# Layer 3 of a four-layer block: its experts' tokens found by ranks and gathers, a pair of experts at a time, in place of a scattered table of token numbers

## The chip, the cores and the metric

The kernel runs on one core of a Trainium2 chip, as one launch. The metric is the device time of that launch in microseconds. The engines of the core run side by side, each with its own queue of instructions executed in order: PE (matmuls; PEld are its weight loads), DVE (vector work), ACT (activations and copies), POOL (the indirect DMAs of this kernel and some elementwise work) and SP (the plain DMAs). Engines wait for each other and for DMAs by semaphores.

## The reference

`x` has 2048 tokens of 256 numbers. Four layers each add a cross-attention and then a feed-forward part, both on a layernorm of `x`. Only the feed-forward part of layer 3 is touched: 16 experts, two per token, each expert with a capacity of 320 tokens.

```python
logits = x_tokens @ router_w + router_b
vals, idx = jax.lax.top_k(jax.nn.softmax(logits, axis=-1), K)        # K = 2
vals = vals / (jnp.sum(vals, axis=-1, keepdims=True) + 1e-09)
oh_e = jax.nn.one_hot(idx.reshape(NK), E, dtype=x.dtype)             # E = 16
pos = (jnp.cumsum(oh_e, axis=0) * oh_e).sum(axis=1) - 1              # place of a pair in its expert
within = (pos < C).astype(x.dtype)                                   # C = 320
expert_inputs = jnp.zeros((E, C, d)).at[idx_flat, pos_c].add(x_pair) # slots of each expert
expert_outputs = jax.vmap(_mlp)(expert_inputs, w_gate, w_up, w_down) # silu(h @ wg) * (h @ wu) @ wd
gathered = expert_outputs[idx_flat, pos_c] * (vals_flat * within)[:, None]
output_tokens = gathered.reshape(N, K, d).sum(axis=1)
return x + _mlp(x, sw_gate, sw_up, sw_down) + output_tokens.reshape(b, s, d)
```

So each of the 16 x 320 slots has to learn which token stands in it, and each token has to learn in which two slots its results are.

## The kernel before

Tokens are handled in four blocks of 512 (`NB`), each of four tiles of 128 (`NT`), so 16 tiles. Activations stay in SBUF; the layernormed tokens of layer 3 are also written to HBM (`xn_dram`, L1449), from where rows can be gathered. Within the attention of every layer the order of PE, DVE and ACT is written out by hand. Outside it, in `ffn3` too, a scheduler orders the instructions of each engine: program order gives the priority, and an instruction that is ready may fill a gap. Tiles come from pools; those with the same tag share a fixed number of buffers, and a new one waits until an old one has been read for the last time. PSUM tiles (`ps_one`, `ps_misc`) share seven buffers. `act` tiles tagged `xnT` share five, `work` six, `xn` one.

The end of the program runs as follows. The last block leaves attention (L355 to L380), is normed on DVE and POOL (L393 to L406), transposed (L416), and its router logits are computed (L621); its routing (L746 to L760, L631, L632) runs on DVE. Then `ffn3`:

- Counting. `both` (L1218) is the one-hot of a token's two experts. Two matmuls count, for each token and expert, the earlier tokens of the same tile (`upper`, L1221) and the totals of each tile (`ones`, L1222). DVE sums the totals over the tiles (L1226), and picks each token's place (`pos`, L1242).
- The table. From the place DVE works out a row in a table of token numbers in HBM (L1250 to L1262), and POOL writes the numbers there with 32 indirect DMAs of 128 rows, one for each tile and choice (L1264). SP reads the table back into `slots` (L1280).
- The shared MLP, `mlp_hidden` (L1305 on PE, Silu on ACT L1309, the product on DVE L1312) and its down projection (L1323, L1331), over the four blocks.
- The experts, one after the other: weights by SP (L1290 to L1293, two buffers each), three gathers of token rows by POOL with `slots` (L1338), six transposes on PE (L1348) with copies on ACT (L1351), `mlp_hidden` on 320 columns, the down projection (L1357), its copy (L1364) and its write to `ys_dram` (L1365).
- The combine: for each tile two gathers from `ys_dram` (L1372), two weighted sums on DVE (L1378), and the result of each block to HBM (L1381).

Layer 1 (`ffn1`) has no table: it writes the ranks of tokens within each tile to HBM, finds for each slot the tile that holds its token from the running totals, gathers that tile's row of ranks, and counts how many are not above the slot's rank (L1002 to L1047).

Of the kernel before, what the change touches and what calls it, by code (L numbers as in the profile page):

```python
# [11 lines left out]
F32 = mybir.dt.float32  # L12
# [54 lines left out]
def block_stack(ctx: ExitStack, tc: tile.TileContext, I: dict, out: bass.AP):  # L67
# [1136 lines left out]
    def ffn3(xnT, chosen, xn_dram):  # L1204
        NTT = NB * NT
        TW = E3 * len(SC)

        table = dram.tile([P * TW, 1], I32, name="table")
        zero = const.tile([P, TW], I32, name="zero")
        nc.vector.memset(zero, 0)  # L1210
        nc.sync.dma_start(table.rearrange("(p c) o -> p (c o)", p=P), zero)
        ids = const.tile([P, NTT], I32, name="ids")
        nc.gpsimd.iota(ids, pattern=[[P, NTT]], base=0, channel_multiplier=1)

        oh, idx, w = chosen

        both = act.tile([P, NTT, E3], F32, tag="mp", name="both")
        nc.vector.tensor_tensor(both, oh[0], oh[1], ALU.add)  # L1218
        bothf = both.rearrange("p t e -> p (t e)")
        pin, ptot = ps_one(), ps_one()  # L1220
        nc.tensor.matmul(pin[:, 0 : NTT * E3], upper, bothf, start=True, stop=True)  # L1221
        nc.tensor.matmul(ptot[:, 0 : NTT * E3], ones, bothf, start=True, stop=True)  # L1222
        base = act.tile([P, NTT, E3], F32, tag="mp", name="base")
        nc.vector.memset(base[:, 0, :], 0.0)
        for t in range(1, NTT):
            nc.vector.tensor_tensor(  # L1226
                base[:, t, :], ptot[:, (t - 1) * E3 : t * E3], base[:, t - 1, :], ALU.add
            )
        before = act.tile([P, NTT, E3], F32, tag="mp", name="before")
        nc.vector.tensor_tensor(  # L1230
            before, pin[:, 0 : NTT * E3].rearrange("p (t e) -> p t e", e=E3), base, ALU.add
        )

        def s16(name):
            return small.tile([P, NTT], F32, tag=name, bufs=1, name=name)

        prod = act.tile([P, NTT, E3], F32, tag="mp", name="prod")
        wk, rows = [], []
        for k in range(2):
            nc.vector.tensor_tensor(prod, before, oh[k], ALU.mult)  # L1240
            pos = s16(f"pos{k}")
            nc.vector.tensor_reduce(pos.unsqueeze(2), prod, AX.X, ALU.add)  # L1242
            within = s16(f"within{k}")
            nc.vector.tensor_scalar(within, pos, float(CAP), None, ALU.is_lt)
            wt = s16(f"wt{k}")
            nc.vector.tensor_tensor(wt, w[k], within, ALU.mult)
            wk.append(wt)

            c1, c2 = s16("c1"), s16("c2")
            nc.vector.tensor_scalar(c1, pos, float(P), None, ALU.is_ge)  # L1250
            nc.vector.tensor_scalar(c2, pos, float(2 * P), None, ALU.is_ge)
            nc.vector.tensor_tensor(c1, c1, c2, ALU.add)
            at = s16(f"at{k}")
            nc.vector.tensor_scalar(at, c1, 1.0 - P * TW, None, ALU.mult)
            nc.vector.scalar_tensor_tensor(at, pos, float(TW), at, ALU.mult, ALU.add)
            nc.vector.scalar_tensor_tensor(at, idx[k], float(len(SC)), at, ALU.mult, ALU.add)
            past = s16("past")
            nc.vector.tensor_scalar(past, within, -1e6, 1e6, ALU.mult, ALU.add)
            nc.vector.tensor_tensor(at, at, within, ALU.mult)
            nc.vector.tensor_tensor(at, at, past, ALU.add)  # L1260
            at_u = small.tile([P, NTT], U32, tag=f"at_u{k}", bufs=1, name=f"at_u{k}")
            nc.vector.tensor_copy(at_u, at)  # L1262
            for t in range(NTT):
                nc.gpsimd.indirect_dma_start(  # L1264
                    out=table,
                    out_offset=bass.IndirectOffsetOnAxis(ap=at_u[:, t : t + 1], axis=0),
                    in_=ids[:, t : t + 1],
                    in_offset=None,
                    bounds_check=P * TW - 1,
                    oob_is_err=False,  # L1270
                )

            row = s16(f"row{k}")
            nc.vector.tensor_scalar(row, pos, float(CAP - 1), None, ALU.min)
            nc.vector.scalar_tensor_tensor(row, idx[k], float(CAP), row, ALU.mult, ALU.add)
            row_u = small.tile([P, NTT], U32, tag=f"row_u{k}", bufs=1, name=f"row_u{k}")
            nc.vector.tensor_copy(row_u, row)
            rows.append(row_u)
        slots = small.tile([P, E3, len(SC)], U32, tag="slots", bufs=1, name="slots")
        nc.sync.dma_start(  # L1280
            slots.rearrange("p e c -> p (e c)"),
            table.rearrange("(p c) o -> p (c o)", p=P).bitcast(U32),
        )
# [12 lines left out]
        def mlp_hidden(gu, xT, n):  # L1296
# [3 lines left out]
            for f, (lo, hi) in enumerate(FC):  # L1300
                fw = hi - lo
                pg = [ps_one("ps_h") for i in range(2)]
                for i in range(2):
                    for c in range(2):
                        nc.tensor.matmul(  # L1305
                            pg[i][0:fw, 0:n], gu[:, i, c, lo:hi], xT[:, c, 0:n], start=(c == 0), stop=(c == 1)
                        )
# [7 lines left out]

        gu, dn = load_mlp("sw")
        for b in range(NB):
            hs = mlp_hidden(gu, xnT[b], BT)
# [14 lines left out]
        ys_dram = dram.tile([E3 * CAP, D], F32, name="ys")  # L1333
        for e in range(E3):
            gu, dn = load_mlp("w", e)
            xg = act.tile([P, len(SC), D], F32, tag="work", bufs=6, name="xg")
            for s, (lo, hi) in enumerate(SC):
                nc.gpsimd.indirect_dma_start(  # L1338
                    out=xg[0 : hi - lo, s, :],
                    out_offset=None,  # L1340
                    in_=xn_dram,
                    in_offset=bass.IndirectOffsetOnAxis(ap=slots[0 : hi - lo, e, s : s + 1], axis=0),
                )
            xT = act.tile([P, 2, CAP], F32, tag="work", bufs=6, name="xT")
            for c in range(2):
                pt = ps_misc()
                for s, (lo, hi) in enumerate(SC):
                    nc.tensor.transpose(  # L1348
                        pt[:, lo:hi], xg[0 : hi - lo, s, c * P : (c + 1) * P], ident[0 : hi - lo, 0 : hi - lo]
                    )  # L1350
                nc.scalar.copy(xT[:, c, :], pt[:, 0:CAP])  # L1351
            hs = mlp_hidden(gu, xT, CAP)
            ys = act.tile([P, len(SC), D], F32, tag="o_tok", bufs=2, name="ys_sb")
            for s, (lo, hi) in enumerate(SC):
                pd = ps_one()
                for f, (flo, fhi) in enumerate(FC):
                    nc.tensor.matmul(  # L1357
                        pd[0 : hi - lo, 0:D],
                        hs[f][:, lo:hi],
# [221 lines left out]
```

## Time and profile before

| | us |
|---|---|
| median of three runs | 4492.72 (4482.02 to 4495.58) |
| profiled execution | 4487.74 |
| its span, first to last instruction | 4486.0 |
| PE busy in the span | 4258.6 (95%) |
| DVE, ACT, POOL busy | 2414.3, 1959.6, 653.1 |
| shared MLP of layer 3 | 4141.5 to 4205.7 |
| first expert's first transpose | 4237.9 |
| combine and output | 4434 to 4486.0 |

A line of the profile names the source line, the engine, the operation, the tile written and the tiles read, their shapes and a count; times are microseconds from the start of the span, durations of a single instruction are in ns where that is said. What stands after a bar or in brackets is the time for which the engine was idle just before, with what ended that idle time. The granted PE clock is a share of full speed. A float32 matmul is two PE instructions; a transpose is one.

### The profile page before, as it was taken

Reading aid. Unit: us, or ns where it says so; the run is one execution under the profiler, and the core shown is the slowest. Engines: PE = TensorE matmul, PEld = TensorE weight load, DVE = VectorE, ACT = ScalarE, POOL = GpSimd, SP = SyncE. Lnnn points to the kernel's source line nnn. Section 1 sums busy time; section 2 is a strip of 40 time slices with the busy share of each in tenths; the row PEclk is TensorE's granted clock in tenths of the full one; section 3 lists DMA queues with packets and bytes.
Section 4 is the critical chain, followed back from the end, with each engine's and each line's share of the span. In section 5 each row is a group of like instructions: output and inputs, shape, how many; then the busy total and the mean of one; then the engine's idle time right before and its main releaser. Section 6 shows DMA issues by size and latency. Waiting matters only on the chain. (4 is left out here: it accounts for less than half of the span.)

```text
span 4486.0 us, 62975 instructions
## 1 busy us (share of the span) xinstructions
PE 4258.6 (95%) x25100; PEld 1965.4 (44%) x25100; DVE 2414.3 (54%) x4911; ACT 1959.6 (44%) x3690; POOL 653.1 (15%) x833
## 2 busy tenths in 40 slices
PE   8999999999999999998996999999999999998695
PEld 4333333366543333336885433334443333333463
DVE  5776776324677776753222544451486777673122
ACT  1666655511156655662221234343016766665010
POOL 2000100100000010004445100012000001001323
PEclk8999999999999999999998799999899999999897
DMA  2000000000000000002453000000000000000144
GB/s 75 3 3 4 3 3 6 3 23 1 3 3 6 4 8 3 11 6 70 163 167 89 10 5 3 5 6 3 3 16 3 4 3 8 11 1 10 32 148 116
DMA packets 64429, 117.31 MB, mean 26 GB/s; under 512 B 20110, under 2 KB 41478, under 8 KB 59528
## 3 DMA queue, kind: packets, MB, share of 16 engines
q1 hardware_dynamic: 43272, 58.12, 4.3%
q0 software_dynamic: 20864, 55.18, 4.1%
q8 instruction: 198, 3.24, 0.3%
q14 instruction: 95, 0.78, 0.1%
HBM read 138.37 MB, written 16.88 MB: 35 GB/s over the span
## 5 line engine op out<-in xcount | busy, mean ns | idle before, releaser
L284 DVE TENSOR_REDUCE mx<-ps_m 128x1 f32<-128x512 f32 x2688 | 1699.9, 685 | 672.2 <-PE ps_m L277 437.5
L325 PE MATMUL ps_s<-q,kT 32*128 32x512 f32 (+2 forms) x5824 | 1721.0, 623 | 0.7 <-DVE mx L284 0.6
L277 PE MATMUL ps_m<-kT,q 32*128 32x512 f32 x5376 | 1604.8, 644 | 29.9 <-DMA q<-qc 18.5
L335 ACT ACTIVATE e<-ps_s 128x512 f32<-128x512 f32 (+1 forms) x2080 | 1110.7, 599 | 890.5 <-PE ps_s L325 694.4
L343 PE MATMUL ps_acc<-e,V 128*32 128x512 f32 (+2 forms) x5824 | 928.5, 609 | 6.2 <-ACT a L524 5.7
L325 PEld LDWEIGHTS ps_s<-q,kT 32*128 32x128 f32 (+2 forms) x5824 | 576.4, 180 | 671.7 <-DVE mx L284 397.0
L277 PEld LDWEIGHTS ps_m<-kT,q 32*128 32x128 f32 x5376 | 580.4, 188 | 504.4 <-issue 383.1
L333 ACT ACTIVATE e<-ps_s,mcol 128x512 f32<-128x512 f32 (+1 forms) x832 | 514.8, 686 | 224.3 <-PE ps_s L325 143.8
L343 PEld LDWEIGHTS ps_acc<-e,V 128*32 128x32 f32 (+2 forms) x5824 | 160.6, 112 | 640.6 <-issue 508.4
L266 POOL MEMSET mp<- 128x512 f32 x64 | 33.2, 525 | 1846.7 <-PE ps_m L315 1836.2
L1075 ACT ACTIVATE h<-ps_h,w 128x128 f32<-128x128 f32 x320 | 91.1, 372 | 217.7 <-issue 138.2
L854 DVE SCALAR_TENSOR_TENSOR x<-ps_m,cw,x 128x256 f32<-128x256 f32 x256 | 111.1, 479 | 102.1 <-PE ps_m L846 99.1
L402 POOL TENSOR_SCALAR rs<-mv 128x4 f32<-128x4 f32 x32 | 7.6, 239 | 1050.5 <-DVE mv L394 1050.5
L406 POOL TENSOR_SCALAR xn<-x,mv,rs 128x256 f32<-128x256 f32 x128 | 156.0, 1231 | 3.5
L1067 PE MATMUL ps_h<-xT,w 128*128 128x128 f32 x1280 | 153.2, 279 | 0.4 <-issue 0.4
L817 ACT ACTIVATE h<-ps_h 128x512 f32<-128x512 f32 x80 | 47.7, 597 | 242.3 <-PE ps_h L816 242.3
L1067 PEld LDWEIGHTS ps_h<-xT,w 128*128 128x128 f32 x1280 | 149.6, 195 | 0.8 <-issue 0.5
L301 DVE TENSOR_REDUCE mx<-ps_m 128x4 f32<-128x260 f32 x224 | 80.4, 423 | 126.0 <-PE ps_m L293 126.0
L1089 PE MATMUL ps_m<-w,h 128*128 128x256 f32 x640 | 144.6, 379 | 0.0
L1089 PEld LDWEIGHTS ps_m<-w,h 128*128 128x128 f32 x640 | 118.6, 190 | 14.5
L1312 DVE TENSOR_TENSOR h<-ps_h,sg 128x320 f32<-128x320 f32 (+3 forms) x60 | 31.8, 530 | 168.1 <-PE ps_h L1305 121.6
L816 PE MATMUL ps_h<-xnT,up 128*128 128x512 f32 x256 | 117.9, 604 | 0.0
(286 smaller groups left out, 3179.6 us busy)
## 6 DMA issues: line engine op xcount, KB each, us to landing
q<-qc SPq DMA_DIRECT2D x192, 32.0 KB
gu<-in_w_gate SPq DMA_DIRECT2D x16, 352.0 KB
gu<-in_w_up SPq DMA_DIRECT2D x16, 352.0 KB
ys_dram<-ys SPq DMA_DIRECT2D x40, 128.0 KB
xn_dram<-xn SPq DMA_DIRECT2D x8, 512.0 KB
dn<-in_w_down SPq DMA_DIRECT2D x16, 256.0 KB
ys<-ys_sb SPq DMA_DIRECT2D x32, 128.0 KB
x<-in_x SPq DMA_DIRECT2D x4, 512.0 KB
```

Source lines behind the costliest of these rows:

```text
L277: nc.tensor.matmul(pm, q1[at : at + 32, t * P : (t + 1) * P], kT[at : at + 32, g, KB[kb] : KB[kb + 1]], start=True, stop=True,)
L284: nc.vector.tensor_reduce(mx[:, t, j, kb : kb + 1], pm, AX.X, ALU.max)
L325: nc.tensor.matmul(sp, kT[j * S : (j + 1) * S, g, c * P : c * P + cw], q2[j * S : (j + 1) * S, :], start=True, stop=True,)
L333: nc.scalar.activation(e[0:cw], sp, AF.Exp, bias=mcol[0:cw, c : c + 1])
L335: nc.scalar.activation(e[0:cw], sp, AF.Exp)
L343: nc.tensor.matmul(acc[j * S : (j + 1) * S, :], V[0:cw, c, h * (d + 1) : h * (d + 1) + S], es[j // 2][0:cw, j % 2, :], start=(c == 0), sto ...
L406: nc.gpsimd.tensor_scalar(xn[:, t, :], x[b][:, t, :], mv[:, t, 0:1], rs[:, t : t + 1], ALU.subtract, ALU.mult)
L816: nc.tensor.matmul(pu, u(c), xnT[b][:, c, :], start=(c == 0), stop=(c == 1))
L854: nc.vector.scalar_tensor_tensor(x[b][:, t, :], pd[:, i * D : (i + 1) * D], cws[b][:, t, e0 + e + i : e0 + e + i + 1], x[b][:, t, :], ALU. ...
L1067: nc.tensor.matmul(pu[:, (f - f0) * P : (f - f0 + 1) * P], w1[:, c * F1 + f * P : c * F1 + (f + 1) * P], xT[:, c, :], start=(c == 0), stop ...
L1075: nc.scalar.activation(h[:, f, :], pu[:, (f - f0) * P : (f - f0 + 1) * P], AF.Gelu, bias=w1[:, 2 * F1 + f : 2 * F1 + f + 1],)
L1089: nc.tensor.matmul(pd[:, 0:D], h[:, f, :], w2[:, f * D : (f + 1) * D], start=(f == 0), stop=(f == 7))
```

## The change

The table, its 32 scatters, the slots and their arithmetic go. All small tiles are cut from one tile `pad3`, which takes the buffer of layer 3's values (`V`). The counting moves into `counts()`, which also makes the rank of every token in its tile and expert (128 ranks for each of 256 pairs of tile and expert) and writes them to HBM. The 5120 slots are seen as 40 columns of 128, five columns for each pair of experts, the middle column half and half. `locate()` finds for all of them at once the tile and the rank within it; `fetch_ranks(k)` gathers the rank rows of pair k, five indirect DMAs; `tokens(k)` counts along them and gives token numbers; `pairs(k)` gathers the tokens, again five indirect DMAs; `pairs_T` transposes them. These steps stand between the blocks of the shared MLP and then run ahead inside a loop over eight pairs of experts. Each token's own place and weight (`places`) are worked out after experts 3 and 5. The combine and the loads of weights stay as they were.

```diff
     SC = [(0, P), (P, 2 * P), (2 * P, CAP)]
     def ffn3(xnT, chosen, xn_dram):
-        NTT = NB * NT
-        TW = E3 * len(SC)
-        table = dram.tile([P * TW, 1], I32, name="table")
-        zero = const.tile([P, TW], I32, name="zero")
-        nc.vector.memset(zero, 0)
-        nc.sync.dma_start(table.rearrange("(p c) o -> p (c o)", p=P), zero)
-        ids = const.tile([P, NTT], I32, name="ids")
-        nc.gpsimd.iota(ids, pattern=[[P, NTT]], base=0, channel_multiplier=1)
...
         oh, idx, w = chosen
+        vw = 16 * (D // 16 + 1)
+        pad, used = big.tile([P, NCH, vw + P // 4 - D // 16 - 1], F32, tag="V", name="pad3"), 0
+        pad = pad.rearrange("p c n -> p (c n)")
...
+        bothf = cut(NE)
+        nc.vector.tensor_tensor(by_tile(bothf), oh[0], oh[1], ALU.add)
+        ranks_dram = dram.tile([NE, P], F32, name="ranks3_dram")
+        ranks, cum, before = cut(2 * P), by_tile(cut(NE)), by_tile(cut(NE))
+        def counts():
+            for k in range(2):
+                prow, at = ps_one(), slice(k * P, (k + 1) * P)
+                nc.tensor.matmul(prow[:, 0:P], bothf[:, at], upper, start=True, stop=False)
+                nc.tensor.matmul(prow[:, 0:P], bothf[:, at], ident, start=False, stop=True)
+                nc.scalar.copy(ranks[:, at], prow[:, 0:P])
+                nc.sync.dma_start(ranks_dram[at, :], ranks[:, at])
+            ptot, pin = ps_one(), ps_one()
+            nc.tensor.matmul(ptot[:, 0:NE], ones, bothf, start=True, stop=True)
+            nc.tensor.matmul(pin[:, 0:NE], upper, bothf, start=True, stop=True)
+            tot, pin = by_tile(ptot[:, 0:NE]), by_tile(pin[:, 0:NE])
+            nc.vector.tensor_copy(cum[:, 0, :], tot[:, 0, :])
+            for t in range(1, NTT):
+                nc.vector.tensor_tensor(cum[:, t, :], tot[:, t, :], cum[:, t - 1, :], ALU.add)
+            nc.vector.tensor_copy(before[:, 0, :], pin[:, 0, :])
+            nc.vector.tensor_tensor(before[:, 1:, :], pin[:, 1:, :], cum[:, :-1, :], ALU.add)
+        PARTS = [
+            (slice(0, 2), slice(0, P), 0),
+            (slice(2, 3), slice(0, HP), 0),
+            (slice(2, 3), slice(HP, P), 1),
+            (slice(3, 5), slice(0, P), 1),
+        ]
+        rank, tile_of, last, row = (cut(NC) for _ in range(4))
+        row_u, tok_u = cut(NC, U32), cut(NC, U32)
+        gone, cumt = cut(NC * NTT), cut(NC * NTT)
...
+        nc.vector.tensor_copy(rank, slot_id[:, 0:NC])
+        for k in range(E // 2):
+            for cs, ps_, two in PARTS:
+                cols = slice(5 * k + cs.start, 5 * k + cs.stop)
+                nc.gpsimd.tensor_scalar(
+                    rank[ps_, cols], slot_id[ps_, cols], float(-CAP * (2 * k + two)), None, ALU.add
+                )
+                nc.gpsimd.memset(row[ps_, cols], float(2 * k + two))
+        def locate():
+            g4 = gone.rearrange("p (k c t) -> p k c t", c=5, t=NTT)
+            c4 = cumt.rearrange("p (k c t) -> p k c t", c=5, t=NTT)
+            cum4 = cum.rearrange("p t (k two) -> p two k t", two=2)
+            for cs, ps_, two in PARTS:
+                n = cs.stop - cs.start
+                shape = [ps_.stop - ps_.start, E // 2, n, NTT]
+                nc.vector.tensor_tensor(
+                    g4[ps_, :, cs, :],
+                    cum4[ps_, two].unsqueeze(2).to_broadcast(shape),
+                    fives(rank)[ps_, :, cs].unsqueeze(3).to_broadcast(shape),
+                    ALU.is_le,
+                )
+                nc.vector.tensor_tensor(
+                    c4[ps_, :, cs, :],
+                    cum4[ps_, two].unsqueeze(2).to_broadcast(shape),
+                    g4[ps_, :, cs, :],
+                    ALU.mult,
+                )
+            g3 = gone.rearrange("p (c t) -> p c t", t=NTT)
+            c3 = cumt.rearrange("p (c t) -> p c t", t=NTT)
+            nc.vector.tensor_reduce(tile_of.unsqueeze(2), g3, AX.X, ALU.add)
+            nc.vector.tensor_reduce(last.unsqueeze(2), c3, AX.X, ALU.max)
+            nc.vector.tensor_tensor(rank, rank, last, ALU.subtract)
+            nc.vector.tensor_scalar(tile_of, tile_of, NTT - 1.0, None, ALU.min)
+            nc.vector.scalar_tensor_tensor(row, tile_of, float(E), row, ALU.mult, ALU.add)
+            nc.vector.tensor_copy(row_u, row)
+        def fetch_ranks(k):
+            rk = act.tile([P, 5, P], F32, tag="xn", bufs=1, name="rk")
+            for c in range(5):
+                nc.gpsimd.indirect_dma_start(
+                    out=rk[:, c, :],
+                    out_offset=None,
+                    in_=ranks_dram,
+                    in_offset=bass.IndirectOffsetOnAxis(ap=row_u[:, 5 * k + c : 5 * k + c + 1], axis=0),
+                )
+            return rk
+        def tokens(k, rk):
+            at = slice(5 * k, 5 * k + 5)
             nc.vector.tensor_tensor(
...
+                rk, rk, rank[:, at].unsqueeze(2).to_broadcast([P, 5, P]), ALU.is_le
             )
+            tok = tmp([5], "tok5")
+            nc.vector.tensor_reduce(tok.unsqueeze(2), rk, AX.X, ALU.add)
+            nc.vector.scalar_tensor_tensor(tok, tile_of[:, at], float(P), tok, ALU.mult, ALU.add)
+            nc.vector.tensor_scalar(tok, tok, T - 1.0, None, ALU.min)
+            nc.vector.tensor_copy(tok_u[:, at], tok)
+        def pairs(k):
+            xg = [act.tile([P, n, D], F32, tag="xnT", bufs=5, name="xg") for n in (3, 2)]
+            xg = [xg[c // 3][:, c % 3, :] for c in range(5)]
+            for c in range(5):
+                nc.gpsimd.indirect_dma_start(
+                    out=xg[c],
+                    out_offset=None,
+                    in_=xn_dram,
+                    in_offset=bass.IndirectOffsetOnAxis(ap=tok_u[:, 5 * k + c : 5 * k + c + 1], axis=0),
+                )
+            return xg
+        def pairs_T(xg):
+            xT = [wide("xT")[:, 0 : 2 * CAP] for c in range(2)]
+            for c in range(2):
+                for lo, hi in ((0, 4), (4, 5)):
+                    pt = ps_misc()
+                    for col in range(lo, hi):
+                        nc.tensor.transpose(
+                            pt[:, (col - lo) * P : (col - lo + 1) * P], xg[col][:, c * P : (c + 1) * P], ident
+                        )
+                    nc.scalar.copy(xT[c][:, lo * P : hi * P], pt[:, 0 : (hi - lo) * P])
+            return xT
+        def places(k):
...
+            nc.vector.tensor_scalar(wt, pos, float(CAP), None, ALU.is_lt)
+            nc.vector.tensor_tensor(wt, w[k], wt, ALU.mult)
+            nc.vector.tensor_scalar(row_k, pos, float(CAP - 1), None, ALU.min)
+            nc.vector.scalar_tensor_tensor(row_k, idx[k], float(CAP), row_k, ALU.mult, ALU.add)
+            nc.vector.tensor_copy(row_ku, row_k)
+            return wt, row_ku
...
                         nc.tensor.matmul(
-                            pg[i][0:fw, 0:n], gu[:, i, c, lo:hi], xT[:, c, 0:n], start=(c == 0), stop=(c == 1)
+                            pg[i][0:fw, 0:n], gu[:, i, c, lo:hi], xT[c][:, 0:n], start=(c == 0), stop=(c == 1)
...
+        rks, xgs = {}, {}
         gu, dn = load_mlp("sw")
         for b in range(NB):
-            hs = mlp_hidden(gu, xnT[b], BT)
+            if b == 1:
+                counts()
+                locate()
+                rks[0] = fetch_ranks(0)
+            elif b == 2:
+                tokens(0, rks.pop(0))
+                xgs[0] = pairs(0)
+                rks[1] = fetch_ranks(1)
+            elif b == 3:
+                tokens(1, rks.pop(1))
+            hs = mlp_hidden(gu, [xnT[b][:, c, :] for c in range(2)], BT)
...
-        ys_dram = dram.tile([E3 * CAP, D], F32, name="ys")
-        for e in range(E3):
-            gu, dn = load_mlp("w", e)
...
+        ys_dram = dram.tile([E * CAP, D], F32, name="ys")
+        prods = cut(NE)
+        found = {}
+        for k in range(E // 2):
+            xT = pairs_T(xgs.pop(k))
+            if k + 1 < E // 2:
+                xgs[k + 1] = pairs(k + 1)
+            if k + 2 < E // 2:
+                rks[k + 2] = fetch_ranks(k + 2)
+            for two in range(2):
+                e = 2 * k + two
+                gu, dn = load_mlp("w", e)
+                hs = mlp_hidden(gu, [xT[c][:, two * CAP : (two + 1) * CAP] for c in range(2)], CAP)
+                ys = act.tile([P, len(SC), D], F32, tag="o_tok", bufs=2, name="ys_sb")
...
+                if two == 0 and k + 2 < E // 2:
+                    tokens(k + 2, rks.pop(k + 2))
+                if e in (3, 5):
+                    found[(e - 3) // 2] = places((e - 3) // 2)
```

## The prediction

> **What bounds the kernel now.** I first read the busy time by stage of the end of the kernel: the last attention steps, the shared MLP of layer 3, the wait, the experts, the combine. Columns: stretch, its length, then busy us (and instructions) of PE, PEld, DVE, ACT and POOL, the granted PE clock, DMA share, GB/s.
>
> ```profile
> 4115.00:4141.00 26.00, 12.75 (x55) 9.90 (x56) 8.24 (x47) 4.34 (x7) 8.46 (x7) 0.72 0.06 20
> 4141.00:4206.00 65.00, 64.72 (x194) 35.83 (x193) 20.51 (x70) 7.15 (x12) 21.52 (x22) 0.98 0.04 12
> 4206.00:4238.00 32.00, 0.09 (x1) 0.10 (x2) 0.45 (x1) 0.00 (x0) 12.38 (x13) 0.54 0.07 18
> 4238.00:4434.00 196.00, 194.12 (x768) 126.14 (x768) 43.56 (x96) 34.46 (x80) 42.39 (x46) 0.98 0.45 130
> 4434.00:4486.00 52.00, 0.00 (x0) 0.00 (x0) 15.74 (x33) 0.00 (x0) 30.91 (x32) 0.53 0.41 123
> ```
>
> PE fills the shared MLP and the experts; between them it does nothing for 32 us. PE's own timeline shows both holes around the change (start, us, line, then idle before and what ended it):
>
> ```profile
> 4130.78 3.66 PE L621 MATMUL ps_m<-wr,xnT 128*128 128x16 f32 x16 [0.46 <-ACT xnT L417]
> 4139.69 1.19 PE L1221 MATMUL ps_m<-both,upper 128*128 128x256 f32 x2 [5.25 <-DVE base L1224]
> ...
> 4141.53 11.51 PE L1305 MATMUL ps_h<-xnT,gu 128*128 128x512 f32 x24
> ...
> 4200.11 5.61 PE L1323 MATMUL ps_m<-dn,h 128*128 128x256 f32 x24
> 4237.91 0.69 PE L1348 MATMUL ps_m<-ident,xg 128*128 128x128 f32 x2 [32.18 <-DMA xg<-xn_dram,slots]
> ```
>
> What PE waits for is on POOL: 32 scatters into the table, each begun only when the one before has landed, some 2.4 us apart (4150 to 4231), then the read-back of the slots, then the gather.
>
> ```profile
> 4227.73 0.97 POOL L1264 DMA_INDIRECT table<-ids,at_u  x1 [1.40 <-DMA table<-ids,at_u]
> 4230.07 0.97 POOL L1264 DMA_INDIRECT table<-ids,at_u  x1 [1.38 <-DMA table<-ids,at_u]
> 4234.68 1.01 POOL L1338 DMA_INDIRECT xg<-xn_dram,slots  x1 [3.64 <-DMA slots<-table]
> ```
>
> The chain that ended last gives one steady expert, all PE: 1.15 + 6.70 + 4.09 = 11.93 us.
>
> ```profile
> 4254.43 1.15 PE ps_m L1348 x6
> 4255.57 6.70 PE ps_h L1305 x24
> 4262.27 4.09 PE ps_m L1357 x18
> ```
>
> Last, layer 1 already finds tokens by ranks and gathers, so prices for the new work stand in this trace:
>
> ```profile
> L1028 POOL DMA_INDIRECT rk<-ranks_dram,pad x40: 942/964/975, 2077.3 to 2359.6; - x40
> L1034 DVE TENSOR_TENSOR rk<-rk,pad x10: 691/692/694, 2086.9 to 2365.1; 128x512 f32<-128x512 f32 x10
> L1038 DVE TENSOR_REDUCE tok<-rk x10: 674/686/686, 2087.6 to 2366.1; 128x4 f32<-128x512 f32 x10
> ```
>
> **The Trainium skill.** "DMA: Bandwidth & Descriptors", Anatomy of one DMA, puts about 2.0 us of fixed cost, mostly completion, on a DMA that POOL issues; the scatters land in 2.07 us, agreed. The same page, Two DMAs through the same engine are not ordered: a dependent DMA must wait for the first one's semaphore. That is the 1.40 us wait before each scatter, since all write one table; gathers into different columns carry none (issues 1.25 us apart in the combine). "TensorE: Matmul & The Clock Gate", Part 1: an idle PE drops to half clock until about 3.4 us of activity; the trace grants 0.54 in the hole.
>
> **The change part by part.** Measured from the span of 4486.0 us.
>
> Hole before the shared MLP. Today the two count products L1221 and L1222 stand ahead of block 0 on PE and wait 5.25 us for the routing of the last block. After, `counts()` stands behind block 0 in program order, which PE follows in this stage. Block 0 then starts when L621 ends, 4134.4, instead of 4141.5. Its inputs are there: the weights were issued at 3328, xnT of block 0 is old, and ACT's Silu table (4136.8) is in before the first product pair is finished (4134.4 + 3.5). A block costs 15.75 us warm (L1305 starts at 4158.32, 4174.07, 4189.81); block 0 took 16.8 and I keep 0.5 of that 1.05 for a cold clock.
>
> `counts()` on PE. Four rank products of 128 columns, two instructions each: 8 x 0.12 (L1067: 153.2 us for 1280 instructions of 128 columns) = 1.0; two of 256 columns, 4 x 0.227 (4.09 / 18) = 0.9. So 1.9 us. The shared MLP ends at 4134.4 + 4 x 15.75 + 0.5 + 1.9 = 4199.9, instead of 4205.7.
>
> Hole after it. The gap is gone if the first pairs have landed by 4199.9. Counts end at 4152.6. DVE: 16 sums of 16 columns 3.1 (15 took 3.09) and `before`; 4155.8. `locate()`: eight tensor_tensor, 4 x 0.42 (as L1240, 128x256) + 4 x 0.29 (as L640, 128x128) = 2.8; two reductions over 640, (640+151)/0.96 = 0.82 each (estimate by "VectorE: DVE Perf Modes", TRN2 errata; it gives 0.69 at 512, as the trace has); six small ones 1.0; 4161.3. In the same time ACT copies two rank rows (0.3 each), and SP, idle from 4130 to 4200, writes them; the weights of expert 1 stand behind them there, first due at 4195. `fetch_ranks(0)`: five gathers 1.25 apart, the last landing 3.1 after its start (chain: xg 4237.26, 3.10 us): 5.0 + 3.1 = 8.1; 4169.7. `tokens(0)`: 2 x 0.82 + 3 x 0.17 = 2.2; `pairs(0)`: 8.1; landed near 4180.5, 19 us early. Layer 1 needs 36 us from `both` (2057.9) to its first transposes (2093.6); from 4150.7 that is 4187, still early. So the 32.2 us go. What is removed from the chain is POOL's 80 us of scatters (32 x 2.4, a few longer), SP's read-back (1.63) and some 30 DVE instructions of 0.17 between 4147 and 4151.5; only the hole of it was on PE's path, the rest lay under the shared MLP. Expert 0 also ran cold and waited 1.0 for its third gather: 4237.9 to 4254.4 = 16.5 against 11.93, another 4.5 us.
>
> Experts. Transposes fall from 12 to 10 per pair, 0.19 each (1.14/6): a pair costs 10 x 0.19 + 2 x (6.70+4.09) = 23.48 instead of 23.87; eight pairs 187.8, ending at 4387.7. Cover for the rest: POOL 10 gathers per pair, 12.5 us of 23.5 (now 6, 7.5 us); DVE `tokens` 2.2 us per pair, `places` twice some 2 us, while DVE is 22% busy there. PE stays busy as long as h is ready by L1357, 4.5 us after it could be. Weights are issued at the end of L1305 of the expert two before, 17 us ahead of use, and the DMA traffic of one expert lasts some 9 of its 12 us. Without cover each us is paid once per pair.
>
> Sixty-four small POOL writes into `rank` and `row`. No row shows them at this shape; nearest are a 2x16 memset 0.12 and a 128x4 tensor_scalar 0.23, so 8 to 15 us. They need layer 3's V freed (4115). Behind the residual add (4132) they cost 0. If the scheduler puts all ahead of rs (4123.3), into POOL's 8.3 idle us, they delay the last xn by up to 7 us; not below 0. I take 0.
>
> DVE beside the shared MLP: about 14 us added, 2 at most spilling to PE in one block (h waits, seven PSUM buffers). I take 1 for it and the experts' first pair together. The combine keeps its 32 gathers: 52.2 us.
>
> Sum: end of the shared MLP 4205.7 to 4199.9 (start -7.1, cold clock -0.6, counts +1.9) -5.8; hole -32.2; expert 0 -4.5; transposes -3.1 (8 x 0.39); friction +1: -44.6, say -45. Span 4441. The execution took 4487.74, 1.7 more than its span, so 4443; the median of the runs shown is 5 us above it. Against the mean of all four (4489.5) it is 4444.5, against the median 4447.7; I say 4446.
>
> **Rivals.**
> A, more. PE also pulls block 0 into its idle 4121.3 to 4126.0, ahead of L416: 4.7 us more, 4441. Against: now too nothing ready is pulled there or into the 5.25 us.
>
> B, part given back. POOL's small writes ahead of rs (up to 7), DVE late with h at each of three blocks (2 each), PSUM waits in `pairs_T`, which takes four buffers at once (1 per pair): up to 20 back, 4452 to 4470. For: DVE fills gaps out of program order. Against: it has 70% free.
>
> C, slower. DVE runs in order; `tokens(k+2)` stands between the two experts of a pair and can hold up the odd expert's h while ranks are on their way. Layer 1 shows DVE waiting for ranks 52.6 us in 9 waits (5.8 each), though PE isn't held there. Up to 3.5 us late costs nothing; beyond it each us costs six (tokens 2 to 7). It eats the 45 when ranks come 7.5 + 3.5 = 11 us late, i.e. 24 us after the pair's start. Even if POOL starts both groups only at that start, they land after 10 x 1.25 + 3.1 = 15.6, 3 us after the even expert ends. At 14 us late: 6 x 10.5 = 63 lost, 45 won, some 4509.
>
> D, no effect. The small tiles are all cut from one tile; if gathers that read one column held DVE's writes to the next, the chain would slip: the first 19 us are free, then each costs one, and 19 + 45 = 64 us of slip end at some 4491. Layer 1 cuts its tiles the same way and doesn't slip.
>
> **How the numbers follow.** Forecast 0.74 (own range 4434 to 4456, run spread of +-6 included), A 0.06, B 0.11, C 0.05, D 0.04. Range 4432 to 4464: the forecast, A and half of B. 0.3% of 4490 is 13.5 us, about what a measurement can tell from no change. Faster 0.91, same 0.04 (D), slower 0.05 (C).
>
> **What would show it.** L1305 of block 0 straight after L621 with no 5 us hole; POOL with no chained scatters, rank gathers of pair 0 near 4162 to 4170; first expert transposes within 1 us of the last L1323, granted clock near 1.0 there; pairs 23.5 us apart; combine 52 us. Wrong if PE waits over 5 us before the experts, or odd experts' L1357 wait for DVE.

## The result, and the profile after

The changed kernel takes 4495.99 us (median of 20, 4490.11 to 4509.57) against 4487.9 us (20 runs, 4476.28 to 4496.36) for the kernel before: a ratio of 1.0021, 95% interval 1.0012 to 1.0030. It is 8 us slower, where 45 us less were forecast (4446 us). The loss is small, though the interval leaves out 1; the gain isn't there at all, and the forecast is wrong. The profiled execution has a span of 4488.4 us.

Spans differ by some us between executions before the part that was changed is reached. So stages are compared from one mark, the start of the last attention value product (L343), at 4113.05 in the trace of before and 4107.59 after. From there to the end before takes 372.95 us and after 380.81: 7.9 us more, the same as the medians say.

Busy time by stage of the changed kernel: stretch, its length, busy us (and instructions) of PE, PEld, DVE, ACT and POOL, granted PE clock, DMA share, GB/s. The first four rows are blocks 0 to 3 of the shared MLP, then pairs 0 and 1, pairs 2 to 7, the combine.

```profile
4134.50:4151.00 16.50, 16.50 (x47) 9.20 (x48) 7.09 (x38) 3.33 (x5) 0.00 (x0) 0.91 0.01 1
4152.80:4169.10 16.30, 15.75 (x50) 8.80 (x49) 13.35 (x49) 1.79 (x3) 4.15 (x5) 1.00 0.12 20
4169.10:4200.70 31.60, 18.45 (x50) 10.70 (x49) 7.36 (x15) 1.79 (x3) 16.63 (x18) 0.78 0.39 53
4200.70:4231.00 30.30, 19.46 (x49) 10.97 (x48) 7.53 (x15) 1.79 (x3) 14.40 (x16) 0.77 0.47 65
4231.00:4277.00 46.00, 28.61 (x108) 17.93 (x105) 12.10 (x28) 5.44 (x14) 22.93 (x26) 0.85 0.53 104
4277.00:4437.00 160.00, 159.55 (x646) 107.80 (x646) 39.58 (x90) 26.78 (x66) 17.71 (x19) 0.99 0.46 130
4437.00:4488.40 51.40, 0.00 (x0) 0.00 (x0) 15.82 (x33) 0.00 (x0) 30.56 (x32) 0.54 0.43 124
```

The stage of 32 us in which PE did nothing is gone, but blocks 2 and 3 take twice their 15.75 us and pairs 0 and 1 are long too. In those stretches DVE is busy for a quarter of the time. It isn't short of time; it stands still. PE's timeline of the changed kernel (start, us, line, idle before and what ended it) says for what PE waits:

```profile
4124.63 0.69 PE L416 MATMUL ps_m<-ident,xn 128*128 128x128 f32 x2 [7.71 <-POOL xn L406]
...
4193.57 7.27 PE L1414 MATMUL ps_m<-dn,h 96*128 96x256 f32 x20 [13.15 <-DVE h L1392]
...
4221.63 1.22 PE L1414 MATMUL ps_m<-dn,h 128*128 128x256 f32 x2 [10.06 <-DVE h L1392]
...
4231.06 1.25 PE L1346 MATMUL ps_m<-ident,xg 128*128 128x128 f32 x10
...
4254.62 4.83 PE L1441 MATMUL ps_m<-dn,h 96*128 96x256 f32 x10 [12.05 <-DVE h L1392]
...
4277.16 7.88 PE L1385 MATMUL ps_h<-xT,gu 128*128 128x320 f32 x22 [3.81 <-DVE ys_sb L1448]
```

The fourth line is the step forecast: the experts' first transposes follow the shared MLP without a gap. The second, third and fifth wait for `h`, the product of DVE behind which the down projection stands. The sixth waits for a PSUM buffer, which DVE's copy of the results of expert 1 (L1448) frees. The first, for xn, comes last below. DVE's own timeline in block 2 shows why `h` is late:

```profile
4176.25 1.29 DVE L1392 TENSOR_TENSOR h<-ps_h,sg 128x512 f32<-128x512 f32 x2
...
4190.56 0.82 DVE L1318 TENSOR_TENSOR rk<-rk,pad 128x640 f32<-128x640 f32 x1 [13.03 <-DMA rk<-ranks_dram,pad]
...
4192.82 0.69 DVE L1392 TENSOR_TENSOR h<-ps_h,sg 96x512 f32<-96x512 f32 x1
```

The third `h` of block 2 stands behind L1318, the first instruction of `tokens(1)`, and that waits 13.03 us for rank gathers. The inputs of that `h` were there at 4179.5. In the source `tokens(1)` stands after block 2; the scheduler put it between the second and the third `h` of that block. All eight, `tokens(0)` to `tokens(7)`, begin between 4173.6 and 4276, while the source has the last one in pair 5. The list of waits of the changed kernel from 4110 on (waiting for what: us in total, times, longest):

```profile
DVE rk L1318 <- DMA rk<-ranks_dram,pad: 64.9, 8, 13.7
...
PE ps_m L1414 <- DVE h L1392: 24.5, 4, 13.2
...
PE ps_m L1441 <- DVE h L1392: 12.1, 1, 12.1
```

These waits for `h`, the 3.81 us for the copy and 1.5 us for another such buffer make 41.9 us of PE's time. The rest of the 54 us lost against the ordered run below is a lower clock: it was 0.77 to 0.85 in blocks 2 and 3 and pairs 0 and 1, and 20 products took 7.27 us in block 2 where 24 took 5.61 in block 0. Once the eighth is done the pairs follow each other every 22.83 us (23.48 forecast). Last, POOL's timeline of the changed kernel, on the small writes:

```profile
4109.55 3.00 POOL L1273 MEMSET pad<- 128x2 f32 x32 [0.25 <-PE ps_acc L343]
...
4113.13 8.68 POOL L1270 TENSOR_SCALAR pad<-slot_id 64x1 f32<-64x1 f32 x30 [0.20 <-POOL pad L1270]
4121.89 0.23 POOL L402 TENSOR_SCALAR rs<-mv 128x4 f32<-128x4 f32 x1
```

They stand ahead of `rs` of the last block, which sets xn and so L416.

### The profile page after: what moved, and what is told of

The parts are those of the page before. It is cut to its first block, busy times and chain, and to the rows that moved or that the text cites. A ratio compares the mean times of both kernels' runs of the same rounds, so it can differ in the third digit from the quotient of the medians.

```text
span 4488.4 us, 63027 instructions
## 1 busy us (share of the span) xinstructions
PE 4257.7 (95%) x25092; PEld 1972.4 (44%) x25092; DVE 2431.6 (54%) x4946; ACT 1956.7 (44%) x3692; POOL 660.1 (15%) x896
## 5 line engine op out<-in xcount | busy, mean ns | idle before, releaser
L343 PE MATMUL ps_acc<-e,V 128*32 128x512 f32 (+2 forms) x5824 | 925.4, 608 | 5.7 <-ACT a L524 5.7
L343 PEld LDWEIGHTS ps_acc<-e,V 128*32 128x32 f32 (+2 forms) x5824 | 159.9, 112 | 635.5 <-issue 505.7
L846 PE MATMUL ps_m<-dn,h 128*128 128x256 f32 x512 | 117.3, 382 | 0.0
```

Source lines behind the costliest of these rows:

```text
L343: nc.tensor.matmul(acc[j * S : (j + 1) * S, :], V[0:cw, c, h * (d + 1) : h * (d + 1) + S], es[j // 2][0:cw, j % 2, :], start=(c == 0), sto ...
L846: nc.tensor.matmul(pd[:, i * D : (i + 1) * D], h[:, i, t * P : (t + 1) * P], dn[:, e + i, :], start=True, stop=True,)
```

## The experiments

The theory, T: the loss is one of order on DVE's queue. Each `tokens(k)` that stands ahead of an `h` due earlier makes that `h`, and PE, wait for gathers that nothing else needs so soon. Rival W: DVE's added work (or PSUM) is what costs. Rival G: the rank gathers are slow, or held to one buffer's round trip, wherever `tokens(k)` stands. Stages measured from the mark, one profiled execution each, in us:

| | mark to experts | experts to end | mark to end | against after |
|---|---|---|---|---|
| before | 124.9 | 248.1 | 372.95 | -7.9 |
| after | 123.5 | 257.3 | 380.8 | |
| ordered on DVE | 92.5 | 234.0 | 326.5 | -54.3 |
| ordered in the blocks alone | 110.1 | 269.3 | 379.4 | -1.4 |
| ordered in the pairs alone | 109.4 | 234.3 | 343.6 | -37.2 |
| no rank gathers | 93.2 | 232.2 | 325.4 | -55.4 |
| second rank buffer | 134.3 | 233.9 | 368.2 | -12.6 |
| ordered on POOL | 111.2 | 283.4 | 394.6 | +13.8 |
| ordered, tokens(2) early | 104.7 | 234.0 | 338.7 | -42.1 |
| ordered, no small writes | 89.3 | 234.2 | 323.5 | -57.3 |

### Program order on DVE

```diff
+        with tc.manual_schedule(engines={mybir.EngineType.DVE}):
             for b in range(NB):
...
+        with tc.manual_schedule(engines={mybir.EngineType.DVE}):
             for k in range(E // 2):
```

> The changed kernel, but VectorE keeps program order in the shared MLP loop and in the loop over pairs, so tokens(k) stands where the source has it and not ahead of h products that are due earlier. Theory T (order): the 31 us lost in blocks 2 and 3 and the 23 us lost in pairs 0 and 1 come from h standing in VectorE's queue behind a tokens(k) whose ranks are still on their way. Then PE's waits for h (24.5 us at L1414, 12.1 us at L1441 in the changed kernel) fall below 4 us together, blocks take 16 us, every pair 22.8 to 23.5 us, and the time is 4435 to 4455 us, 0.988 to 0.992 of before. Rival W (VectorE's added work or PSUM): the same work is still there, blocks 2 and 3 keep about 30 us, 4488 to 4500. Rival G (the gathers are slow wherever tokens stands): about half of the waits stay, 4465 to 4490.

Measured: 4436.98 us, 0.9893 of before (0.9876 to 0.9909). All instructions are those of the changed kernel; DVE's order differs, and with it how POOL's gathers of ranks and of xg mix. Its stages from block 0 on:

```profile
4136.30:4152.85 16.55, 16.55 (x47) 9.19 (x48) 7.09 (x38) 3.33 (x5) 0.00 (x0) 0.90 0.01 1
4154.60:4170.40 15.80, 15.80 (x49) 8.69 (x48) 11.23 (x35) 1.79 (x3) 4.19 (x5) 1.00 0.13 20
4170.40:4186.15 15.75, 15.75 (x49) 8.82 (x48) 5.49 (x10) 1.79 (x3) 8.02 (x9) 1.00 0.38 57
4186.15:4201.90 15.75, 15.75 (x49) 8.77 (x48) 5.49 (x10) 1.79 (x3) 8.47 (x10) 1.00 0.45 85
4201.90:4224.65 22.75, 22.73 (x95) 15.43 (x93) 7.78 (x17) 4.03 (x10) 8.21 (x10) 1.00 0.62 151
4224.65:4384.40 159.75, 159.61 (x659) 108.41 (x658) 51.61 (x123) 28.19 (x70) 46.98 (x50) 1.00 0.59 147
4384.40:4435.90 51.50, 0.10 (x1) 0.00 (x0) 15.93 (x33) 0.00 (x0) 30.41 (x32) 0.54 0.44 126
```

PE is full in every stage before the combine, at full clock from block 1 on, and no wait of PE for `h` is left. `tokens(1)` still waits 4.81 us for its ranks, and the first two `h` of block 3 stand behind it, but they are done at 4195.4, and PE comes to their down projection at 4196.5, a margin of 1 us; from `tokens(2)` on the ranks have landed before DVE arrives. DVE's timeline of this kernel in pair 0:

```profile
4214.04 0.42 DVE L1450 COPY ys_sb<-ps_m 64x256 f32<-64x256 f32 x1 [1.01 <-PE ps_m L1443]
4214.38 0.81 DVE L1318 TENSOR_TENSOR rk<-rk,pad 128x640 f32<-128x640 f32 x1
...
4216.62 0.49 DVE L1392 TENSOR_TENSOR h<-ps_h,sg 128x320 f32<-128x320 f32 x1
```

W wanted all the waits to stay and G half of them; both fall. All 54.3 us lost against this run, 30.9 in the shared MLP and 23.4 in the pairs, were lost to the order on one engine.

### Without the rank gathers

```diff
-            for c in range(5):
-                nc.gpsimd.indirect_dma_start(
-                    out=rk[:, c, :],
...
-                rk, rk, rank[:, at].unsqueeze(2).to_broadcast([P, 5, P]), ALU.is_le
+                rk, ranks[:, 0:P].unsqueeze(1).to_broadcast([P, 5, P]), rank[:, at].unsqueeze(2).to_broadcast([P, 5, P]), ALU.is_le
```

> Leaves out the 40 rank gathers: tokens(k) compares rows of ranks that lie in SBUF already, the same 128x640 comparison, so the token numbers are other ones. VectorE's work is unchanged, and the scheduler may place it as it likes (it puts all eight tokens(k) among blocks 1 to 2). Theory T: no wait of VectorE for a DMA between the counts and the experts; h is late only by the 18 us of token work that stand ahead of it, of which at most 10 reach PE in blocks 1 and 2; pairs 22.8 us each; 4435 to 4460. Rival W: PE waits for h as in the changed kernel, 20 us or more in the blocks, 4480 to 4500. Rival G: as T, so that this run tells W alone apart.

Measured: 4439.68 us, 0.9900 (0.9884 to 0.9917). DVE does the same token work, all eight pulled ahead once more, without anything to wait for. PE's wait for `h` in the list of waits of this kernel:

```profile
PE ps_m L1407 <- DVE h L1385: 0.8, 1, 0.8
```

So token work placed early is harmless; what costs is a token step that waits. That rules W out a second time, and by another way than the order.

### A second buffer for the ranks

```diff
-            rk = act.tile([P, 5, P], F32, tag="xn", bufs=1, name="rk")
+            rk = act.tile([P, 5, P], F32, tag="xn", bufs=1, name="rk") if k % 2 == 0 else gone.rearrange(
+                "p (c n) -> p c n", c=5
+            )
```

> The ranks of odd pairs land in a second buffer (the 640 columns of gone, free after locate()), so that the rank gathers of pair k+1 need not wait for tokens(k). The scheduler now puts all eight tokens(k) ahead of the last h product of block 3. Theory T: a second buffer doesn't mend it: the last h of block 3 stands behind tokens(7), whose ranks land no sooner than 4163.7 + 40 x 1.25 + 3.7, about 4218 and with five gathers of xg among them 4224; the experts start about 4230, as in the changed kernel, but then all pairs take 22.8 us; 4468 to 4480, PE's wait for h in the shared MLP 20 to 30 us. Rival G (the single buffer's round trip is what costs): the waits halve, experts start by 4215, 4450 to 4465. Rival W: 4490 to 4500.

Measured: 4479.11 us, 0.9985 (0.9977 to 0.9992), at the upper edge of what T expected and far from G's. The usual cure for a single buffer gives back 12.6 of 54 us. The trace shows it making the shared MLP longer (134.3 us from the mark to the experts, against 123.5) and the pairs clean. All eight `tokens(k)` now stand ahead of the last `h` of block 3, and PE waits there until the 40 rank gathers have gone through POOL one by one. PE's timeline of this kernel:

```profile
4226.82 1.22 PE L1416 MATMUL ps_m<-dn,h 128*128 128x256 f32 x2 [14.03 <-DVE h L1394]
4232.59 1.22 PE L1416 MATMUL ps_m<-dn,h 128*128 128x256 f32 x2 [4.55 <-DVE h L1394]
4239.06 7.70 PE L1416 MATMUL ps_m<-dn,h 96*128 96x256 f32 x20 [5.25 <-DVE h L1394]
4246.60 1.26 PE L1348 MATMUL ps_m<-ident,xg 128*128 128x128 f32 x10
```

The expectation had the experts start near 4230; they start at 4246.60 (4241.9 when moved to the mark of after). It counted five gathers of xg among the 40 of ranks, and POOL's timeline has ten (6.3 us more); of the other 5.6 us the down projection behind the waits has about 3, on a granted clock of 0.58 (7.70 us for 20 products); the rest I haven't traced.

### Order in one of the two loops

For the blocks alone:

```diff
+        with tc.manual_schedule(engines={mybir.EngineType.DVE}):
             for b in range(NB):
```

For the pairs alone:

```diff
+        with tc.manual_schedule(engines={mybir.EngineType.DVE}):
             for k in range(E // 2):
```

> VectorE keeps program order in the shared MLP loop alone; the loop over pairs is left to the scheduler, which still puts tokens(2) to tokens(7) ahead, two of them among the h of block 3, the others among pairs 0 and 1. Theory T: blocks 1 and 2 at 16 us, block 3 and pairs 0 to 1 still held up by tokens(2) to (7), whose 30 rank gathers on POOL take 1.25 us each and share it with those of xg; some 25 to 35 us of the 54 come back, 4460 to 4475, about 0.996 of before. Rival W: no change, 4490 to 4500. Rival G: no change, since the gathers are as slow as before, 4485 to 4500.

> VectorE keeps program order in the loop over pairs alone; in the shared MLP loop the scheduler orders it. It now has only tokens(0) and tokens(1) to pull ahead, and puts tokens(1) between the first and the second h of block 2, where the changed kernel has it just behind the second. Theory T, order: block 2 loses what it lost in the changed kernel, 31.6 - 15.75 = 16 us, blocks 1 and 3 take about 16, all pairs 22.8; 4450 to 4457, the fully ordered run plus 16. If instead it is the number of tokens(k) placed early that counts, 2 of 8, it costs 2/8 of 54, that is 13, and from one run of times the two can't be told apart, but the wait in block 2 tells. Rival G, gathers slow wherever tokens stand: refuted by the ordered run, expects no more here.

Measured: blocks alone 4490.84 us, 1.0015 (1.0008 to 1.0022); pairs alone 4459.86 us, 0.9934 (0.9910 to 0.9959). For the blocks alone the expectation of T was wrong: not half of the loss came back, but 1.4 us of 54. The stages gained 13.4 us in the shared MLP and lost 12.0 in the pairs. The reason is in the place of the last step that was pulled ahead: `tokens(7)` begins 168.4 us after the mark in the changed kernel (4275.94) and 172.8 here (4280.68); in both the eight follow one another through POOL and the one rank buffer. In both something that PE needs for expert 2 stands behind it: in the changed kernel the copy of L1448, here the third `h` of expert 2. PE's timeline of this kernel in pair 1:

```profile
4281.95 5.68 PE L1442 MATMUL ps_m<-dn,h 96*128 96x256 f32 x12 [11.37 <-DVE h L1392]
```

PE can't get past that, so what it doesn't lose before, it loses in front of it. I had priced the waits one by one, as if each could be taken away alone. By its time alone this run is what W and G foretold; its trace isn't. Blocks 1 and 2 take 16.7 and 15.75 us (block 2 of the changed kernel took 31.6), and the loss stands in block 3 and pairs 0 and 1, where the token steps are out of place.

For the pairs alone, T's size was right and the number of the table says so: 17.1 us above the ordered run from the mark (16 expected; the median is 3 us above the expected range). Only `tokens(1)` is out of place, and block 2 takes all of it. PE's timeline of that kernel:

```profile
4197.44 1.22 PE L1414 MATMUL ps_m<-dn,h 128*128 128x256 f32 x2 [12.94 <-DVE h L1392]
4199.44 6.93 PE L1414 MATMUL ps_m<-dn,h 96*128 96x256 f32 x20 [0.78 <-DVE h L1392]
```

### One token step put ahead by hand

Against the ordered version, at the start of block 3:

```diff
                     tokens(1, rks.pop(1))
+                    tokens(2, fetch_ranks(2))
...
-                if k + 2 < E // 2:
+                if 0 < k < E // 2 - 2:
                     rks[k + 2] = fetch_ranks(k + 2)
...
-                    if two == 0 and k + 2 < E // 2:
+                    if two == 0 and 0 < k < E // 2 - 2:
                         tokens(k + 2, rks.pop(k + 2))
```

> The ordered version, and one tokens(k) put ahead by hand: fetch_ranks(2) and tokens(2) stand at the start of block 3 instead of in pair 0. All else, the work too, is the same. Theory T: tokens(1) frees the rank buffer at 4193.8 (times of the ordered run), five gathers take 6.25 us, the last lands 3.1 after its start, so tokens(2) begins near 4203 and the first h of block 3 follows at 4205.5 instead of 4190; PE has its 24 products of L1385 done at 4196.5 and waits 9 to 10 us at L1415, and runs some 2 us longer on a clock gone cold; 4446 to 4450, 0.9915 to 0.9925 of before. If a single tokens(k) ahead is harmless (the loss is one of the total load): 4437.

Measured: 4447.79 us, 0.9906 (0.9890 to 0.9923), and 12.2 us more than the ordered run from the mark. This is the mechanism made on purpose, with a size foretold. DVE's and PE's timelines of this kernel:

```profile
4210.55 0.82 DVE L1318 TENSOR_TENSOR rk<-rk,pad 128x640 f32<-128x640 f32 x1 [9.15 <-DMA rk<-ranks_dram,pad]
...
4212.81 1.88 DVE L1392 TENSOR_TENSOR h<-ps_h,sg 128x512 f32<-128x512 f32 x3
```

```profile
4213.56 7.68 PE L1416 MATMUL ps_m<-dn,h 128*128 128x256 f32 x24 [9.99 <-DVE h L1392]
```

PE waits 9.99 us (9 to 10 expected), and then needs 7.68 us for 24 products that take 5.61 in the ordered run: 2.1 us of a lower clock (granted 0.70) on top of the wait, 12.1 together.

### Program order on POOL instead

Against the ordered version, in both loops:

```diff
-        with tc.manual_schedule(engines={mybir.EngineType.DVE}):
+        with tc.manual_schedule(engines={mybir.EngineType.Pool}):
```

> The changed kernel with program order on POOL, not on VectorE, in the two loops: the five rank gathers of a pair stand together, then the five of xg, in place of ranks and xg in among each other. The scheduler still orders VectorE and puts tokens(1) ahead of the last h of block 2, tokens(2) ahead of all h of block 3, tokens(3) and on ahead of the last h of every other expert. Theory T: the waits move with the places of tokens(k): about 11 us in block 2, 10 to 15 in block 3, up to 10 in pair 0, little after it since ranks come every 17 us and a pair lasts 22.8; 4457 to 4475. Rival P (the mixed order of POOL's gathers is what makes the ranks late): with ranks together the waits nearly vanish, 4435 to 4447.

Measured: 4504.09 us, 1.0040 (1.0026 to 1.0053), worse than every other version. P, by which the mixed order of POOL's gathers makes the ranks late, falls, and T's number was 30 us too low. T was wrong on the places too: PE waits 14.7 us in block 2 (about 11 expected), block 3 loses 1.5 (10 to 15 expected), and then each of the pairs 0 to 4 takes 32.0 to 33.5 us instead of 22.8. POOL's timeline of this kernel in pair 1 (its transposes start at 4253.05), and DVE's after it:

```profile
4254.42 0.94 POOL L1332 DMA_INDIRECT xg<-xn_dram,pad  x1 [12.65 <-PE ps_m L1346]
4255.66 0.94 POOL L1332 DMA_INDIRECT xg<-xn_dram,pad  x1 [0.30 <-issue]
4256.91 0.94 POOL L1307 DMA_INDIRECT rk<-ranks_dram,pad  x1 [0.30 <-issue]
```

```profile
4267.21 0.83 DVE L1318 TENSOR_TENSOR rk<-rk,pad 128x640 f32<-128x640 f32 x1 [7.65 <-DMA rk<-ranks_dram,pad]
...
4268.80 0.48 DVE L1392 TENSOR_TENSOR h<-ps_h,sg 96x320 f32<-96x320 f32 x1
```

In program order the ranks of pair k+2 stand on POOL behind the xg gathers of pair k+1, and two of those wait for a buffer that the transposes of pair k free. So the ranks can't start before the pair does, and land some 14 us into it, and the scheduler has put `tokens(k+2)` ahead of the third `h` of the even expert, whose inputs are there 8 us into it. I had let the ranks come every 17 us and left that wait for a buffer out.

### The small POOL writes

Against the ordered version, four instructions at the start of the program for 64 in `ffn3`:

```diff
...
+    for cs, ps_, two in ((slice(0, 2), slice(0, P), 0), (slice(2, 3), slice(0, P // 2), 0),
+                         (slice(2, 3), slice(P // 2, P), 1), (slice(3, 5), slice(0, P), 1)):
+        nc.gpsimd.iota(e5[ps_, :, cs], pattern=[[2, E3 // 2], [0, cs.stop - cs.start]], base=two, channel_multiplier=0)
...
-        for k in range(E // 2):
-            for cs, ps_, two in PARTS:
-                cols = slice(5 * k + cs.start, 5 * k + cs.stop)
-                nc.gpsimd.tensor_scalar(
-                    rank[ps_, cols], slot_id[ps_, cols], float(-CAP * (2 * k + two)), None, ALU.add
-                )
-                nc.gpsimd.memset(row[ps_, cols], float(2 * k + two))
```

> The ordered version (program order on VectorE in both loops), and besides the expert number of each slot column comes from four POOL iotas at the start of the program; the 64 small POOL writes into rank and row (11.7 us on POOL, ahead of rs of the last block) and one copy are gone. If these writes held the last xn up, as the changed kernel's trace suggests, the stretch from the last L343 to the first of the last L416 transposes shrinks by 3.0 to 4.2 us and the time is 3 to 4 us below the ordered version's 4437: 4432 to 4435, 0.988 to 0.9885 of before. If they were hidden: no change, 4437.

Measured: 4436.66 us, 0.9884 (0.9867 to 0.9901): by time not to be told from the ordered version. The trace has the step: the last L343 to the first of the last block's L416 (L353 and L426 in this kernel) is 14.07 us against 17.04, and from the mark the whole is 3.0 us shorter. POOL is idle again ahead of `rs` in this kernel:

```profile
4123.05 0.23 POOL L412 TENSOR_SCALAR rs<-mv 128x4 f32<-128x4 f32 x1 [11.27 <-DVE mv L404]
```

This version and the ordered one both beat the kernel before, by some 50 us.

## Why the prediction was wrong

**Hole before the shared MLP: right.** Block 0 follows L621; its first two products even run between those of L621 (4129.85). Counts on PE took 1.76 us (1.9). The lower clock cost more than the 0.5 that were kept: block 0 runs at 0.91.

**Hole of 32.2 us: right.** The transposes follow the shared MLP at once in every version. The chain under it was longer than forecast without reaching the path: in the ordered version 9.3 us from the last count to the rows of `locate()` (8.7 forecast) and 9.9 from the first rank gather to `tokens(0)` (8.1). Rival D, a slip through the shared tile, didn't come, nor A: PE pulled only those two products ahead.

**Experts and combine: right, a little better.** A pair takes 22.82 us, not 23.48, as ten transposes take 1.25 to 1.3 us. The 0.19 each came from 1.15 us for six, and part of that doesn't grow with their number; the likely part, the wait for ACT's copy, wasn't tested. The combine takes 51.5 us (52.2).

**Small POOL writes: the size was right, the place wrong.** The bound was 0 to 7, and 0 was taken. They went ahead of `rs`, 11.7 us on POOL, and L416 is 4.1 us later from the mark, of which the version without them has 3.0 back. The other 1.1 us is the clock before L416: from the mark to the end of L380 the kernel before took 8.2 us at a granted 1.00, the version without the writes 9.3 at 0.82. With the writes in place that clock doesn't matter: the run with a second rank buffer has 1.00 there too, and its L416 comes 17.04 us after the mark, as at 0.82.

**The step that failed is the cover for `tokens`**: "PE stays busy as long as h is ready by L1357, 4.5 us after it could be", and "DVE beside the shared MLP: about 14 us added, 2 at most spilling to PE", together priced at 1 us. It cost 54. The step set DVE's work (2.2 us a token step) against DVE's idle time, and DVE's work was harmless, as the run without rank gathers shows. What it left out is that a queue stands still on an instruction that waits. Against rival B it said that DVE has 70% free; those 70% were of no use while the queue stood. The Trainium skill states the order in "PSUM — Partial Sum Buffer", Engine vs sequencer instructions: the queues of ScalarE, VectorE and GpSimd "are strict FIFO". The trace agrees: DVE stood 13.03 us, the last 11 of them in front of an `h` whose inputs were there. The prediction's own sign of being wrong came in its first half, PE waiting over 5 us before the experts; in the second half it looked at odd experts, and the `h` held up was that of expert 0.

**Rival C had the mechanism and the arithmetic, but took the source's order for the queue's.** It let `tokens(k+2)` stand between two experts and found 3.5 us to spare there. In that place, in the ordered version, the ranks are never late. But the prediction itself noted, under B, that DVE fills gaps out of program order; where the scheduler would take `tokens(k)` to be ready wasn't asked. In the run with POOL in order, C came true in such a place. It let ranks land 15.6 us after a pair's start at the latest; there they are in 15.5 us after that of pair 0 (4219.56 to 4235.02), though by another sum (two gathers of xg, five of ranks, the last of them 6.6 us from its start to DVE's). By C that is harmless, 3 us after the even expert; ahead of that expert's third `h` it cost some 10 us in each of five pairs. C got 0.05, since only one place was tried in it.

**The sum.** From the mark the forecast of -45 is 327.9 us, and the ordered version has 326.5. Its terms: +5.7 before the experts (4.1 by the late L416; the rest, by the granted 0.90 in block 0, a lower clock), -5.3 for the cheaper pairs, -0.7 for the combine, -1 for friction that isn't there. That the sum comes so close is partly luck: 5.7 too little and 7.0 too much cancel. What the chance of 0.74 stood for was this kernel in another order of DVE.

**What stays open:** why the scheduler counts `tokens(k)` as ready so early. In the run with a second rank buffer they moved further ahead, with POOL in order further back, as they would if it gave the gathers too short a time; but no run shows its reckoning. Nor do the runs say why the granted clock before L416 is 1.00 in two of the ten traces and 0.82 in the others.

## What to carry to other kernels

An instruction costs its queue the time that it stands there, not the time that it works: before a step that waits for a DMA is priced by the idle share of its engine, look for what stands behind it and when that is due. Where a scheduler orders the queue, the source doesn't tell which neighbour that is; either the order is written out around the wait, as with two lines here (54 us), or the step is priced at its worst place. And several such waits on one queue can't be priced singly: what counts is when the last of them is over and what stands behind it.

## What the runs showed of the hardware

- Rank gathers begin 1.25 us apart on POOL, as priced, but land a median of 3.7 us after issue in the changed kernel and 4.4 in the ordered one, against the 3.1 that was read from one gather of the kernel before, in the hole. In the ordered one the DMA share is 0.6 in the pairs, in that hole 0.07; that the load is the cause wasn't tested.
- 32 writes of 1 or 2 columns by memset took 3.00 us of POOL, but 30 additions of the same shapes 8.68 us: 0.09 and 0.29 us each.
- A wait of 10 us on PE cost 12: the 24 products behind it took 7.68 us, at a granted 0.70, in place of 5.61.
